# A four-layer graph-attention stack on one core: inverse roots moved to ScalarE, masks planned later, setup products moved to GpSimd

## The chip, the cores and the metric

One Trainium2 chip, of which the kernel uses one core. The metric is the device time of one execution in microseconds (us); the time of a kernel is the median of its runs.

## The reference

128 graphs of 128 nodes go through four attention layers. Each layer is added to its input and normalised over the 512 features. All numbers are float32.

```
def _layernorm(x, axis=-1, eps=1e-5):
    m, v = jnp.mean(x, axis, keepdims=True), jnp.var(x, axis, keepdims=True)
    return (x - m) / jnp.sqrt(v + eps)

# x: (128, 128, 512), adj: (128, 128, 128) of 0 and 1
x = _layernorm(x + L0(x, adj, ...))   # one head: scores x.w_src + x.w_dst + b, softmax over neighbours, attn @ x
x = _layernorm(x + L1(adj, x, ...))   # 4 heads of 256: xl = x @ W1, softmax, + b1, elu; then one head of 512 with W2, + b2
x = _layernorm(x + L2(x, adj, ...))   # 8 heads of 64: h = x @ W, softmax, attn @ h
x = _layernorm(x + L3(x, adj, ...))   # one head: scores from x @ W_fc.T, softmax, elu(attn @ x)

# an attention, e.g. of layer 3
scores = leaky_relu(f1[:, :, None] + f2[:, None, :], 0.2)
scores = where(adj == 0, -1e9, scores)
h_prime = einsum('bnm,bmi->bni', softmax(scores, axis=2), x)
```

## The kernel before

One graph is one tile: its 128 nodes lie on the 128 partitions. A graph passes through some 70 operations in `first`, `second`, `halves` and `third`, and up to sixteen graphs are under way at once. Two passes set the order. `Pipeline.plan` gives each operation of a graph a time, modulo a period of 28 us; graph g's operations get that time plus 28 g. `Pipeline.order` then merges all graphs and the setup into one list: it walks through the operations with one clock for each engine, takes the operation that can start first by the costs written in the code and by `FLOW`, and looks at most 30 us ahead. `FLOW` says how long after its end an operation's result may be read, by the same engine and by others. What is emitted is a fixed order for each engine (PE, DVE, ACT, POOL, and SP for the DMAs); at run time each engine takes its instructions in that order and waits on semaphores. Buffers are placed, and numbered, as the list is emitted.

The steps that the text below speaks of:

- Adjacency matrices are loaded by SP. `mask` turns one into -2^100 or 0 on POOL (L738): m0 for layer 0 (from `ae`, adjacency plus the unit matrix, L838), m2 for layer 2, m3 for layer 3. PE transposes m2 (L850) and DVE multiplies it by `noneye` (L851), which makes m1 for layer 1.
- `spread` writes one column of scores to DRAM and reads it back to all partitions. `attend` takes it: Prelu on ACT (L641), masked scores with the negated maximum nm on DVE (L649), exponential with its sum rs on ACT (L658), reciprocal ri on DVE (L666). `turned` transposes by 32x32 blocks on DVE (L602) and a DMA through DRAM (scr).
- `mixed` is attention times features on PE (L725); L896 and L938 are the same for the four and the eight heads. `resid` adds the input on DVE (L733).
- `project` is a product with weights on PE (L710), w1s with four blocks of 258 columns and wha with two of 273; ACT or DVE evicts PSUM (L717, L715). `halves` multiplies by W2 for two graphs at once with seven products in place of eight (sums on POOL L780, PE L794, evictions L807 on ACT and L812 on DVE).
- `norm`, four in a graph: mean and variance mv by DVE (L676, L677), the inverse root rd by POOL as an addition and a power (L680, L681). The first normalisation is then one DVE operation (L699). For the other three POOL makes the offset mr = -mean x rd (L688, and L692 where 1 is added) and ACT applies scale and offset (L695).
- The setup loads the weights and makes scores' columns from them: `dot2` (L413 and L466) multiplies and sums rows of W2 on DVE, `dots` (L499, L503) rows of the layer-2 weights, and PE sums the W2 columns (L479). The setup's operations stand in the same list as the first graphs'.

Of the kernel before, what the change touches and what calls it, by code (L numbers as in the profile page):

```python
# [17 lines left out]
P = 128  # L18
# [11 lines left out]

PERIOD = 28.0
LATENCY = {"PE": (0.0, 0.8), "DVE": (0.15, 1.6), "ACT": (0.1, 1.6), "POOL": (0.1, 1.6), "SP": (6.8, 6.8)}
FLOW = {"PE": (0.0, 0.6), "DVE": (0.15, 0.9), "ACT": (0.1, 0.9), "POOL": (0.1, 0.9), "SP": (3.2, 3.2)}
AHEAD = 30.0
URGENCY = 0.3
BANKS = 8
# [38 lines left out]
class Pipeline:  # L75
# [69 lines left out]
    def order(self, events):  # L145
# [52 lines left out]
        while len(out) < n:  # L198
            best = None
            for e, waiting in known.items():  # L200
                found = None
                for i in waiting:
                    if events[i][0] > events[low][0] + AHEAD and i != low:
                        break
                    t = start(i)
                    if t is not None and (found is None or t < found[0]):
                        found = (t, i)
                        if t <= clock[e]:
                            break
                if found and (best is None or found < best):  # L210
                    best = found
            t, i = best
            op = ops[i]
            known[op.engine].remove(i)
            issued[i] = True
            out.append((events[i][1], op))
            for b in makes[i]:
                b.slot = free[b.tag].pop(0)[1]
                coming[b.tag].remove(i)
            clock[op.engine] = done = t + op.cost  # L220
            own, other = FLOW[op.engine]
            if op.dma:

                done = lane = max(lane, done) + op.dma
                own = other = FLOW["SP"][0]
            for q in after[i]:
                ready[q] = max(ready[q], done + (own if ops[q].engine == op.engine else other))
                before[q] -= 1
                if not before[q]:
                    insort(known[ops[q].engine], q)  # L230
            for b in op.bufs:
                released[b] = max(released.get(b, 0.0), done + other)
                open_uses[b] -= 1
                if not open_uses[b] and b.slot is not None and b.tag != "const":
                    insort(free[b.tag], (released[b], b.slot))
            while low < n and issued[low]:
                low += 1
# [4 lines left out]
def tile_gat_stack(  # L242
# [44 lines left out]
    nc.vector.tensor_sub(noneye, ones, ident)  # L287
    eye_i = const.tile([P, P], I32, name="eye_i")
    nc.vector.tensor_copy(eye_i, ident)
    neghalf = const.tile([P, 1], F32, name="neghalf")  # L290
    nc.vector.memset(neghalf, -0.5)
    minus = const.tile([P, P], F32, name="minus")
    nc.vector.memset(minus, -1.0)

# [160 lines left out]
        at(40 + s, "PE", 3.5, lambda b=b, f=ones_out: f(b), [w2_marks[0, s], w2_marks[1, s]], [b])  # L455
        at(41 + s, "DVE", 0.33, lambda b=b, f=into: f(b), [b, b2b], [b2b])

    part = const.tile([P, 4], F32, name="part")
    s2 = [spread_row(89, r, 0) for r in r2]
    w2_dots = []  # L460

    def dot2(j, k, s):
        for n in range(2):
            w = w2s[:, SLOT[k // 4, n], k % 4]
            dot(j, w[:, : F // 2], s2[s].ap[:, n * F // 2 : (n + 1) * F // 2], part[:, 2 * s + n : 2 * s + n + 1])
        nc.vector.tensor_add(  # L466
            w2s[:, SLOT[k // 4, s], k % 4, F // 2 : C2], part[:, 2 * s : 2 * s + 1], part[:, 2 * s + 1 : 2 * s + 2]
        )

    for k in range(KH):  # L470
        for s in range(2):
            w2_dots.append(mark())
            j = passing(F)
            at(90 + 2 * k + s, "DVE", 0.9, lambda j=j, k=k, s=s: dot2(j, k, s), [*w2_marks.values(), s2[s]], [j, w2_dots[-1]])

    def shifts(b):
        for s in range(2):
# [15 lines left out]
    at(109.3, "DVE", 1.1, lambda: nc.vector.tensor_sub(w2s[:, 6], w2s[:, 1], w2s[:, 4]), [t2], [t4])  # L493
    w2_ready = [t1, t2, t3, t4]

    def dots(j, k, a, cols):

        pr = j.ap.rearrange("p (h o) -> p h o", h=H2)
        nc.vector.tensor_mul(  # L499
            pr, wha[:, k, :SH].rearrange("p (h o) -> p h o", h=H2)[:, :, :FO],  # L500
            a.ap.rearrange("p (h o) -> p h o", h=H2),
        )
        nc.vector.tensor_reduce(out=wha[:, k, cols], in_=pr, op=ALU.add, axis=AX.X)  # L503

    a3, wf = ([passing(F) for _ in range(2)] for _ in range(2))
    acb, fcp = [passing(P) for _ in range(2)], passing(F)
# [35 lines left out]
    for k in range(KF):  # L542
        for s in range(2):
            for what, cols in ((a3[s], slice(SH + s * H2, SH + (s + 1) * H2)), (wf[s], slice(FO + s, SH, CH))):
                wh_ready.append(mark())
                j = passing(F)
                at(157 + 12 * k + 6 * s, "DVE", 1.2, lambda j=j, k=k, what=what, cols=cols: dots(j, k, what, cols),
                   [*wh_marks[k], what], [j, wh_ready[-1]])

    work = ctx.enter_context(tc.tile_pool(name="work", bufs=1))  # L550
    dram = ctx.enter_context(tc.tile_pool(name="dram", bufs=1, space=bass.MemoryType.DRAM))
# [10 lines left out]
    def graph(g):  # L562
# [107 lines left out]
                ), [zz, ri], [zz])  # L670
            return turned(zz, nh, moving=scaled), ri

        def norm(y, on_act=False, plus=0.0):

            st, mv, rd = small("st", 6), small("mv", 2), small("rd", 1)
            op("DVE", 0.6, lambda: nc.vector.bn_stats(st.ap, y.ap), [y], [st])  # L676
            op("DVE", 0.1, lambda: nc.vector.bn_aggr(mv.ap, st.ap), [st], [mv])  # L677

            def root():
                nc.gpsimd.tensor_scalar_add(rd.ap, mv.ap[:, 1:2], EPS)  # L680
                nc.gpsimd.tensor_tensor(out=rd.ap, in0=rd.ap, in1=neghalf, op=ALU.pow)  # L681

            op("POOL", 0.9, root, [mv], [rd])
            if on_act:
                mr = small("mr", 1)

                def offset():
                    nc.gpsimd.tensor_scalar(  # L688
                        out=mr.ap, in0=mv.ap[:, 0:1], scalar1=rd.ap, scalar2=-1.0, op0=ALU.mult, op1=ALU.mult
                    )  # L690
                    if plus:
                        nc.gpsimd.tensor_scalar_add(mr.ap, mr.ap, plus)  # L692

                op("POOL", 0.6 if plus else 0.3, offset, [mv, rd], [mr])
                op("ACT", 0.6, lambda: nc.scalar.activation(  # L695
                    y.ap, y.ap, AF.Identity, bias=mr.ap, scale=rd.ap
                ), [y, rd, mr], [y])
                return mv, rd
            op("DVE", 0.45, lambda: nc.vector.tensor_scalar(  # L699
                out=y.ap, in0=y.ap, scalar1=mv.ap[:, 0:1], scalar2=rd.ap,  # L700
                op0=ALU.subtract, op1=ALU.mult,
            ), [y, mv, rd], [y])

        def project(lhs, wa, nk, w, t, evict, to, ready):

# [29 lines left out]
            ), [pa, ri, r], [o])  # L735

        def mask(m, a, what):
            op("POOL", 0.8, lambda: nc.gpsimd.tensor_scalar(  # L738
                out=m.ap, in0=a.ap, scalar1=0.0, scalar2=-BIG, op0=what, op1=ALU.mult
            ), [a], [m])  # L740

        def score(xv, wv, init, sc, s):
            jk = Buf("junk", [P, F])
# [167 lines left out]
        def third(g, st, xl2):  # L911
# [6 lines left out]
            pa = mixed(pt, xl2, F)  # L918
            x2 = Buf("x2", [P, F])
            resid(x2, pa, ri, xb)  # L920
            norm(x2, on_act=True)


            xT = turned(x2, KF)
            xl3 = Buf("xl3", [P, C3])
            project(xT, lambda k, c: wha[:, k, c * C3 // 2 : (c + 1) * C3 // 2], KF, C3 // 2, xl3, ["DVE", "ACT"],
                    lambda t, c: t.ap[:, c * C3 // 2 : (c + 1) * C3 // 2], wh_ready)
            db = spread(Col(xl3, SH, H2), H2)
            z3 = Buf("z3", [P, H2, CH])
# [29 lines left out]
                nc.vector.tensor_add(sc4.ap, sc4.ap, xl3.ap[:, C3 - 2 :])  # L959

            op("DVE", 0.2, scores, [z3, xl3], [sc4])
            mv, rd = norm(x3, on_act=True, plus=1.0)

            def normed():

# [18 lines left out]
            ), [e3, pa], [y])  # L984

            op("POOL", 1.3, lambda: nc.gpsimd.tensor_add(y.ap, y.ap, x3.ap), [y, x3], [y])  # L986
            norm(y, on_act=True)
            op("SP", 0.4, lambda: nc.sync.dma_start(out=out[g], in_=y.ap), [y], [], 1.0, dma=0.72)  # L988
        if g == B:

# [60 lines left out]
```

## Time and profile before

| | |
|---|---|
| median of 3 runs | 3205.73 us (3203.74 to 3207.6) |
| profiled execution, own time | 3213.19 us |
| its span, first to last instruction | 3211.2 us |
| mean granted PE clock | 0.980 |
| PE busy (matmuls) | 3050.0 us, 95% |
| DVE busy | 2967.3 us, 92% |
| ACT busy | 2172.0 us, 68% |
| POOL busy | 2285.5 us, 71% |
| DMA, main queue q1 | 75.9% of 16 engines |

Busy times are averages over fill, steady part and drain; the end of a matmul is modelled, so that rows of PE can overlap the next one. Views used below: the list of waits (an engine and line, whom it waited for, total us, times, longest), the table of stretches (busy time of each engine in a stretch of the span), groups by line (count, busy time, mean ns of one), and the timeline (start, length, engine, line, operation).

### The profile page before, as it was taken

To read this page: it belongs to the slowest core of one execution; us is meant where nothing else is said; L and a number is where in the kernel's file an instruction comes from. 1 tells how busy PE (TensorE), PEld (TensorE's weight loads), DVE (VectorE), ACT (ScalarE), POOL (GpSimd) and SP (SyncE) were. 2 spreads that over 40 slices of the span, in tenths; PEclk is the share of its full clock that TensorE was granted. 3 is DMA by queue.
4 is the path that set the end of the run, shared out by engine and by line. 5 is a ranking of instruction groups with operands and counts; after the bars stand their busy time and mean duration, and the time that the engine had idled before them with its cause. 6 is when DMAs were issued, how large, how long until landed. Compare 5 with 4: busy or idle time off the path is not lost. (4 is left out here: it accounts for less than half of the span.)

```text
span 3211.2 us, 62683 instructions
## 1 busy us (share of the span) xinstructions
PE 3050.0 (95%) x14822; PEld 2483.6 (77%) x14822; DVE 2967.3 (92%) x10185; ACT 2172.0 (68%) x7427; POOL 2285.5 (71%) x3211
## 2 busy tenths in 40 slices
PE   7899999999999999999999999999999999999974
PEld 4688877788878878788788787887888878878852
DVE  6978999999999999999999999999999999999985
ACT  1356667677777777777777767777777777777764
POOL 3566777777777777777777777777777777777654
PEclk8999999999999999999999999999999999999985
DMA  4457787787888887888788888887787777878784
GB/s 117 104 147 189 190 196 192 192 202 193 204 192 197 202 194 198 197 197 200 193 198 201 192 203 199 194 204 193 198 200 195 200 197 195 203 190 205 183 192 110
DMA packets 1657572, 606.13 MB, mean 189 GB/s; under 512 B 1311562, under 2 KB 1508170, under 8 KB 1657204
## 3 DMA queue, kind: packets, MB, share of 16 engines
q1 hardware_dynamic: 1655836, 598.97, 75.9%
q8 instruction: 120, 1.97, 0.3%
q14 instruction: 248, 2.03, 0.2%
q0 software_dynamic: 576, 2.10, 0.2%
q10 hardware_dynamic: 792, 1.06, 0.1%
HBM read 374.43 MB, written 227.48 MB: 187 GB/s over the span
## 5 line engine op out<-in xcount | busy, mean ns | idle before, releaser
L658 ACT ACTIVATE w<-w,nm 128x128 f32<-128x128 f32 x1920 | 754.2, 394 | 389.5 <-DVE nm L649 347.3
L710 PE MATMUL ps<-w1s,w 128*128 128x258 f32 x4096 | 940.3, 383 | 7.1 <-DMA w<-scr 7.1
L710 PEld LDWEIGHTS ps<-w1s,w 128*128 128x128 f32 x4096 | 780.7, 191 | 176.8 <-issue 30.0
L794 PE MATMUL ps<-w2s,w 128*128 128x257 f32 x3584 | 872.5, 382 | 8.3 <-POOL w L780 5.8
L649 DVE CUSTOM_DVE_ANT_0 w<-w,w 128x128 f32<-128x128 f32 x1920 | 853.6, 545 | 14.4 <-ACT w L641 12.1
L794 PEld LDWEIGHTS ps<-w2s,w 128*128 128x128 f32 x3584 | 655.7, 190 | 98.1 <-POOL w L780 8.0
L602 DVE STREAM_TRANSPOSE w<-w 128x512 f32<-128x512 f32 (+1 forms) x1024 | 539.2, 540 | 45.9 <-POOL w L668 43.8
L710 PE MATMUL ps<-wha,w 128*128 128x273 f32 x2048 | 518.4, 397 | 4.7 <-DMA w<-scr 4.2
L695 ACT ACTIVATE w<-w,mr,rd 128x512 f32<-128x512 f32 x384 | 311.5, 812 | 298.8 <-POOL mr L688 207.2
L641 ACT ACTIVATE w<-w,xl 128x128 f32<-128x128 f32 x1536 | 480.4, 389 | 35.0 <-DMA w<-row 32.4
L710 PEld LDWEIGHTS ps<-wha,w 128*128 128x128 f32 x2048 | 389.2, 195 | 134.9 <-issue 35.6
L950 POOL TENSOR_TENSOR w<-z,w 128x512 f32<-128x512 f32 x128 | 151.7, 1185 | 348.1 <-DVE z L942 301.1
L680 POOL TENSOR_SCALAR rd<-mv 128x1 f32<-128x1 f32 x512 | 153.3, 299 | 341.2 <-DVE mv L677 184.5
L681 POOL TENSOR_TENSOR rd<-rd,neghalf 128x1 f32<-128x1 f32 x512 | 345.7, 675 | 42.7
L658 ACT ACTIVATION_READ_ACCUMULATOR w<-w,nm 128x1 f32 x1920 | 361.4, 188 | 0.0
L676 DVE BATCH_NORM_STATS2 st<-w 128x6 f32<-128x512 f32 x512 | 340.7, 675 | 10.3 <-POOL w L986 6.3
L717 ACT COPY xl<-ps 128x258 f32<-128x258 f32 (+1 forms) x640 | 226.4, 363 | 153.5 <-PE ps L710 152.7
L881 POOL TENSOR_TENSOR xl<-xl,b1t 128x512 f32<-128x512 f32 x256 | 325.1, 1290 | 0.3
L725 PE MATMUL ps<-w,w 128*128 128x512 f32 x512 | 271.7, 613 | 37.4 <-DMA w<-scr 26.5
L938 PEld LDWEIGHTS ps<-xl,w 128*128 128x128 f32 x2048 | 263.1, 195 | 37.4 <-DVE nm L649 12.8
L649 DVE DVE_READ_ACCUMULATOR2_ANT nm<- 128x1 f32 x1920 | 288.2, 150 | 0.0
L938 PE MATMUL ps<-xl,w 128*128 128x66 f32 x2048 | 256.0, 274 | 18.0 <-DMA w<-scr 11.9
(183 smaller groups left out, 4452.1 us busy)
## 6 DMA issues: line engine op xcount, KB each, us to landing
scr<-w SPq DMA_DIRECT2D x640, 256.0 KB
w<-scr SPq DMA_DIRECT2D x640, 256.0 KB
w<-row SPq DMA_DIRECT2D x128, 512.0 KB
w<-in_x_dram SPq DMA_DIRECT2D x128, 256.0 KB
w<-row SPq DMA_DIRECT2D x128, 256.0 KB
out_dram<-w SPq DMA_DIRECT2D x128, 256.0 KB
w<-row SPq DMA_DIRECT2D x384, 64.0 KB
scr<-w SPq DMA_DIRECT2D x384, 64.0 KB
```

The costliest lines, as they stand in the source:

```text
L602: op("DVE", 0.12 + 0.133 * n, lambda: nc.vector.transpose(zb.ap.rearrange("p b h c -> p h b c"), src.ap.rearrange("p (h b c) -> p h b c", ...
L641: nc.scalar.activation(z.ap[:, h, :], db.ap[:, h0 + h, :], AF.Prelu, bias=src(h0 + h), alpha=SLOPE)
L649: nc.vector.tensor_tensor_reduce(out=zz.ap[:, h, :].rearrange("p (b a) -> p a b", b=4), in0=z.ap[:, h, :].rearrange("p (a b) -> p a b", b= ...
L658: nc.scalar.activation(zz.ap[:, h, :], zz.ap[:, h, :], AF.Exp, bias=nm.ap[:, h : h + 1], scale=-1.0, accum_out=rs.ap[:, h : h + 1],)
L676: op("DVE", 0.6, lambda: nc.vector.bn_stats(st.ap, y.ap), [y], [st])
L681: nc.gpsimd.tensor_tensor(out=rd.ap, in0=rd.ap, in1=neghalf, op=ALU.pow)
L695: op("ACT", 0.6, lambda: nc.scalar.activation(y.ap, y.ap, AF.Identity, bias=mr.ap, scale=rd.ap), [y, rd, mr], [y])
L710: op("PE", w * 4 / 2400 + 0.006, lambda k=k: nc.tensor.matmul(px.ap[:, :w], lhsT=lhs.ap[:, k, :], rhs=wa(k, c), start=(k == 0), stop=(k == ...
L725: op("PE", width * 4 / 2400, lambda: nc.tensor.matmul(pa.ap[:, :width] if len(xv.shape) == 2 else pa.ap.rearrange("p (s c) -> p s c", s=2) ...
L794: return lambda: nc.tensor.matmul(q[b].ap[:, :C2], lhsT=x()[:, k, :], rhs=w2s[:, slot, k, :], start=(fresh and k == 0), stop=(k == 3), ski ...
L881: op("POOL", 1.3, lambda nh=nh: nc.gpsimd.tensor_add(xl.ap[:, nh, : 2 * FH], xl.ap[:, nh, : 2 * FH], b1t[:, nh * 2 * FH : (nh + 1) * 2 * F ...
L938: op("PE", 0.225, lambda u=u, h=h: nc.tensor.matmul(pa.ap[:, u * CH : (u + 1) * CH], lhsT=pt.ap[:, u, :], rhs=xl3.ap[:, h * CH : (h + 1) * ...
```

## The change

- The planner's `FLOW` gives POOL's results to other engines 1.2 us after their end, before 0.9; in `order` an operation on POOL can carry an extra delay, and `mask` carries 2.0 us. The written cost of a mask goes from 0.8 to 0.75.
- `norm` makes the inverse root on ACT as exp(-0.5 ln(var + eps)), two instructions on 128x1, in place of the two on POOL. All four normalisations now take the form with an offset from POOL and an Identity on ACT; `on_act` is gone.
- One table set with both functions is loaded at the start.
- `project` of layer 2 evicts both blocks by ACT.
- In the setup, products of `dot2` and `dots` are made by POOL; the W2 ones are summed by ACT, the others by DVE.

With the number of operations in a graph the planner's random shifts fall on other operations, so the order changes everywhere a little.

```diff
-FLOW = {... "POOL": (0.1, 0.9), ...}
+FLOW = {... "POOL": (0.1, 1.2), ...}
...
             own, other = FLOW[op.engine]
+            if op.engine == "POOL":
+                other += op.extra
...
+    eps = const.tile([P, 1], F32, name="eps")
+    nc.vector.memset(eps, EPS)
+
+    nc.scalar.preload_act_table_set("natural_log_exp_and_others")
...
+    for s in range(2):
+        at(89.5, "ACT", 0.6, lambda s=s: nc.scalar.copy(a2[s].ap, s2[s].ap), [s2[s]], [a2[s]])
     for k in range(KH):
         for s in range(2):
-            at(90 + 2 * k + s, "DVE", 0.9, lambda ...: dot2(j, k, s), [*w2_marks.values(), s2[s]], [j, w2_dots[-1]])
+            at(90 + 2 * k + s, "POOL", 1.3, lambda ...: nc.gpsimd.tensor_tensor(... op=ALU.mult), [*w2_marks.values(), a2[s]], [j])
+            at(91 + 2 * k + s, "ACT", 0.85, lambda ...: nc.scalar.activation(
+                j.ap, j.ap, AF.Copy, accum_out=w2s[:, SLOT[k // 4, s], k % 4, F // 2 : C2]
+            ), [j], [j, w2_dots[-1]])
...
-                at(157 + 12 * k + 6 * s, "DVE", 1.2, lambda ...: dots(j, k, what, cols), [*wh_marks[k], what], [j, wh_ready[-1]])
+                at(157 + 12 * k + 6 * s, "POOL", 1.3, lambda ...: products(j, k, what), [*wh_marks[k], what], [j])
+                at(158.5 + 12 * k + 6 * s, "DVE", 0.65, lambda ...: nc.vector.tensor_reduce(
+                    out=wha[:, k, cols], in_=heads_of(j.ap), op=ALU.add, axis=AX.X
+                ), [j], [wh_ready[-1]])
...
             def root():
-                nc.gpsimd.tensor_scalar_add(rd.ap, mv.ap[:, 1:2], EPS)
-                nc.gpsimd.tensor_tensor(out=rd.ap, in0=rd.ap, in1=neghalf, op=ALU.pow)
-
-            op("POOL", 0.9, root, [mv], [rd])
-            if on_act:
-                ...
-            op("DVE", 0.45, lambda: nc.vector.tensor_scalar(
-                out=y.ap, in0=y.ap, scalar1=mv.ap[:, 0:1], scalar2=rd.ap,
-                op0=ALU.subtract, op1=ALU.mult,
-            ), [y, mv, rd], [y])
+                nc.scalar.activation(rd.ap, mv.ap[:, 1:2], AF.Ln, bias=eps)
+                nc.scalar.activation(rd.ap, rd.ap, AF.Exp, scale=-0.5)
+
+            op("ACT", 0.44, root, [mv], [rd])
+            mr = small("mr", 1)
+            ...
+            op("POOL", 0.6 if plus else 0.3, offset, [mv, rd], [mr])
+            op("ACT", 0.7, lambda: nc.scalar.activation(
+                y.ap, y.ap, AF.Identity, bias=mr.ap, scale=rd.ap
+            ), [y, rd, mr], [y])
...
         def mask(m, a, what):
-            op("POOL", 0.8, lambda: nc.gpsimd.tensor_scalar(
+            op("POOL", 0.75, lambda: nc.gpsimd.tensor_scalar(
                 out=m.ap, in0=a.ap, scalar1=0.0, scalar2=-BIG, op0=what, op1=ALU.mult
-            ), [a], [m])
+            ), [a], [m], 2.0)
...
-            project(xT, lambda k, c: wha[...], KF, C3 // 2, xl3, ["DVE", "ACT"], ...)
+            project(xT, lambda k, c: wha[...], KF, C3 // 2, xl3, ["ACT", "ACT"], ...)
```

## The prediction

> **What bounds the kernel now.** I read the table of stretches first, to separate the steady part from the fill and the drain.
>
> ```profile
> 400.00:800.00 400.00, 387.00 (x1913) 318.16 (x1912) 377.60 (x1297) 280.56 (x963) 295.82 (x421) 1.00 0.80 195
> 800.00:1200.00 400.00, 390.42 (x1934) 320.96 (x1934) 380.27 (x1314) 285.44 (x979) 299.76 (x420) 1.00 0.81 198
> 1600.00:2000.00 400.00, 391.67 (x1935) 321.59 (x1934) 381.87 (x1316) 285.71 (x982) 300.30 (x420) 1.00 0.81 198
> 3100.00:3211.20 111.20, 56.91 (x182) 36.14 (x182) 65.76 (x241) 56.09 (x178) 48.29 (x94) 0.63 0.57 136
> ```
>
> The columns are the stretch, its length, busy us (and instructions) of PE, PEld, DVE, ACT and POOL, the granted clock, the DMA share and GB/s. From 400 to 2800 us nothing changes: PE 98% busy, DVE 95%, ACT 71%, POOL 75%. One step of PE (L725 w<-w,w, timeline) starts at 1600.44 and again, two graphs later, at 1647.80: 47.36 us, so 23.68 us a graph. 128 of them are 3031 us; 180 us are fill and drain.
>
> Who holds PE up comes from the list of waits. The columns are total us, times and longest.
>
> ```profile
> ACT w L658 <- DVE nm L649: 347.3, 421, 12.3
> ACT w L695 <- POOL mr L688: 207.2, 165, 4.4
> PEld ps L850 <- POOL w L738: 111.1, 108, 4.3
> PE ps L850 <- POOL w L738: 61.2, 102, 2.7
> PE ps L725 <- DMA w<-scr: 26.5, 7, 8.8
> ```
>
> The ACT waits are long but ACT has slack. The PE wait is the one that counts: once in nearly every graph the transposition of the mask (L850) waits for the mask from POOL. Asked for 400 to 2800 us alone, PE waited 55.1 us in 94 cases there and under 2 us for everything else together. The timeline of one case, PE and then POOL:
>
> ```profile
> 1625.06 1.02 PE L725 MATMUL ps<-w,w 128*128 128x512 f32 x2
> 1625.91 0.62 PE L710 MATMUL ps<-wha,w 128*128 128x273 f32 x2
> 1626.95 0.33 PE L850 MATMUL ps<-ident,w 128*128 128x128 f32 x1 [0.41 <-POOL w L738]
> 1627.11 1.09 PE L710 MATMUL ps<-wha,w 128*128 128x273 f32 x4
> ```
>
> ```profile
> 1623.83 0.55 POOL L680 TENSOR_SCALAR rd<-mv 128x1 f32<-128x1 f32 x1
> 1624.46 0.57 POOL L681 TENSOR_TENSOR rd<-rd,neghalf 128x1 f32<-128x1 f32 x1
> 1625.12 0.67 POOL L738 TENSOR_SCALAR w<-ae 128x128 f32<-128x128 int32 x1
> 1625.89 0.27 POOL L688 TENSOR_SCALAR mr<-mv,rd 128x1 f32<-128x1 f32 x1
> 1626.23 0.66 POOL L738 TENSOR_SCALAR w<-adj 128x128 f32<-128x128 int32 x1
> ```
>
> POOL works without a break: add, power, the other mask, an offset, then the mask that PE needs, done at 1626.89. PE's twelve L710 matmuls at 1603.09 take 2.76 us, 0.23 each, so the two at 1625.91 end at 1626.37 and PE loses 0.58 us, though the view shows 0.41: the modelled end of a matmul lies about 0.16 us after the next could start. Corrected by that, 102 x (0.60 + 0.16) = **77 us** are lost to this wait. Behind it PE runs at its rate (30 matmuls of 258 columns at 1613.28 in 6.54 us to the next row, 0.218 each), so without it a graph would take about 23.0 us.
>
> **What the Trainium skill says.** "Perfetto Trace Analysis", Identifying the Most-Contended Engine: matmul busy time is a poor measure of distance to the roofline; the trace agrees, the busy 98% hides part of the wait above. "ScalarE: Activation LUTs", What ACT_TABLE_LOAD costs: an ACTIVATE with a pointer bias takes about 280 + 0.833 N ns, with immediates 186, each pointer 93; here 128 elements took 394 (387 by the rule) and 512 with two pointers 812 (800). Its section on table sets says natural_log_exp_and_others holds both exp and ln; no run shows that yet. "SBUF — State Buffer", two separate sides: a GpSimd operation and a VectorE operation with two SBUF inputs exclude each other for a whole instruction; the trace agrees, L649 takes 0.38 us alone and 1.43 at 1607.02 while POOL runs L780.
>
> **The change part by part.**
>
> *Masks reckoned later.* No instruction more or less; the planner takes a mask as 2.0 us (and 0.3) later for other engines. Buffers are numbered as they are placed, about 346 numbers a graph, 0.068 us each. From mask to its PE output there were 26 to 33 numbers (about 2 us) for graphs 20 to 109; in the changed order there are 96 to 154 (6.5 to 10.5 us). POOL would have to run 4 us later against the plan than now for PE to wait. Gain 77 us, less what is late next. PE's other waits are near nothing now, but each had this stop to catch up in; I allow 0.15 us a graph, a fifth of what is removed: 128 x 0.15 = 19, rounded to **15 to 20 back**. Bounds: 0 and all 77.
>
> *Roots to ScalarE.* POOL loses, per graph, 4 x (0.299 + 0.675) = 3.90 us. ACT gains 4 x (Ln 0.281 + Exp 0.187 to 0.281): 1.9 to 2.2 us by the page's price, and Exp waits for Ln, so up to 0.1 more each. No row shows such a pair. Two ACT instructions behind DVE's mv now stand in ACT's order and hold up what follows (exponentials, evictions of PSUM); L695 behind them waits for POOL's offset as before.
>
> *First normalisation on ScalarE.* DVE loses L699, 0.584; ACT gains 0.812 (row L695), POOL an offset, 0.278. *Eviction of xl3*: DVE loses L715, 0.431, ACT gains 0.363 (L717).
>
> Budgets per graph, scaled from 400 to 23.68 us: DVE 22.56 - 1.02 = 21.5; ACT 16.87 + 2.05 + 0.81 + 0.36 = 20.1, up to 20.5; POOL 17.8 - 3.9 + 0.3 = 14.2. Against 23.0 to 23.1 that is 93%, 88%, 62%. PE stays the bound. Without DVE's relief its 22.56 would be 98% of the new period, so that part is worth nothing alone but carries the first. Fewer POOL operations also exclude DVE less; not counted.
>
> *Setup products on POOL.* DVE loses 16 products of w2 (eight stand from 49.19 to 57.29, so 16.2 us in all) and 16 of wha (L499, 1.03 to 1.57: 16 to 25 us). POOL gains 32 of about 1.28 (L862), 41 us; ACT 16 summing passes of about 0.8. PE's L479 needs the last w2 sum and stands ahead of graph 1's projection. Sixteen products and what lies between them (two L862, two masks, sum and offset: 4.6 us) take 25 us from about 48, so L479 opens near 74 where it was served by 69.3. That is **up to 6 us later** for PE; DVE's free 16 us pull graph chains forward by up to as much. Bounds -8 to +8; I take +2. The table load moves from 13.00 to the start, 1.28 us either way: 0, hidden behind the loads of w1.
>
> *Drain.* A norm's chain in the drain changes from add, power (0.23, 0.57 in the chain of work that ended last) to about 0.55 plus one hop: within 3 us, taken as 0.
>
> Sum: -77 + 17 + 2 = -58 on the profiled execution's 3213.2 us; that execution is 7.5 above the median of the runs, so 3205.7 - 58 = 3148; the fill's lean and the lighter POOL are one-sided, I take **3145**.
>
> **The rivals.**
> *ACT becomes the limit (slower, 0.16).* ACT's order is fixed, and of each graph it now idles 23.68 - 16.87 = 6.8 us, mostly waiting for nm (178.6 us in 1600) and mr (160.6). If more than 23.68 - 20.1 = 3.6 us of these waits survive, ACT sets a longer period than now; with 4 us, 24.1 us a graph, 3205.7 + 128 x 0.42 = 3260. For it: four more waits on mv and evictions behind them. Against: the waits exist because ACT is early, and shrink when it is fuller.
> *A new wait takes half (0.12).* A late sum (L794 from POOL) or DVE's 93% costs PE 0.35 us a graph: 3205.7 - 77 + 45 = 3174; at its worst no change (0.06).
> *The change doesn't do what it says.* Were the tables exchanged, eight loads of 1.283 us a graph would add 10 us to ACT. The built order has one load in all, so I give it no chance of its own.
>
> **How the numbers follow.** Likeliest (0.66): 3145, its own range 3110 to 3165. Half gain 0.12, no change 0.06, slower 0.16. Faster 0.78, same 0.06, slower 0.16; 0.2% (6.4 us) is about what a measurement of this kernel can tell from no change. The range 3108 to 3204 leaves out the slower case and little else.
>
> **What would show it.** Right: no row of PE L850 waiting for POOL L738 over 10 us; about 23.1 us between every other L725 of PE; ACT near 87%, DVE near 93%; the sum of PE's waits in 400 to 2800 us under 20. Wrong: ACT over 92% with PE waiting for its evictions (L710 or L938 from ACT), or L850 still waiting; a fill that reaches full rate more than 8 us later.

## The result, and the profile after

The changed kernel takes **3245.14 us** (median of 4 runs, 3239.83 to 3253.06) against 3205.37 us for the kernel before, measured beside it: 1.0126 times as long, 95% interval 1.0099 to 1.0152. The forecast was 3145. Its profiled execution took 3239.83 us with a span of 3237.8, that is 26.6 us over the profiled execution of before; the traces therefore show two thirds of the 39.8 us between the medians, since the one execution lay 5.3 us below its median and the other 7.8 above.

Busy time of the changed kernel, from its page:

```profile
span 3237.8 us, 62168 instructions
PE 3059.5 (94%) x14822; PEld 2501.7 (77%) x14822; DVE 2694.0 (83%) x9833; ACT 2450.4 (76%) x8741; POOL 1902.3 (59%) x2347
```

The work moved as the change says: DVE 273 us and POOL 383 us less, ACT 278 us more. None of the four engines' totals tells why it became slower. The table of stretches, with the columns as in the prediction:

```profile
0.00:400.00 400.00, 359.83 (x1632) 284.07 (x1633) 303.75 (x987) 230.66 (x794) 235.75 (x266) 0.96 0.60 150
800.00:1200.00 400.00, 387.35 (x1914) 321.57 (x1914) 339.73 (x1260) 314.83 (x1128) 242.91 (x301) 0.99 0.80 195
1600.00:2000.00 400.00, 387.39 (x1914) 318.77 (x1912) 337.39 (x1261) 314.07 (x1127) 241.67 (x300) 1.00 0.79 196
```

In the steady part DVE is down to 85%, ACT at 79%, POOL at 60%, and PE is at 387 of 400, where it had 391. No engine but PE is near its limit, and PE's 97% holds waits, as the 98% of before did.

For the **period** one instruction of DVE that occurs once in a graph (L966, sc<-swf,mv,sc) serves as a clock. In before it starts at 718.08 us for the twentieth graph and at 2854.32 for the hundred-and-tenth: 23.74 us a graph. In after it is 715.11 and 2881.28: 24.07. So the twentieth graph comes 3.0 us earlier than before, the ninety graphs after it lose 30 us, and the rest is even. The loss lies in the steady part.

The list of waits of the whole changed kernel (who waited, for whom, total us, times, longest):

```profile
ACT w L646 <- DMA w<-row: 447.7, 261, 6.2
POOL ae L838 <- DMA adj<-in_adj_dram: 275.5, 80, 11.8
DVE w L654 <- ACT w L646: 145.1, 126, 5.3
```

and of PE alone between 400 and 2800 us:

```profile
PE ps L710 <- DMA w<-scr: 35.8, 28, 3.2
PE ps L710 <- DVE nm L654: 13.4, 7, 4.3
PE ps L710 <- DVE w L903: 5.8, 3, 2.6
```

L850, which stood first in the prediction, has 2.1 us left. None of it is for the mask. PE's waits there are 73.7 us in all. About half are for DMAs, and most stand at the third layer's projection (L710), for its transposed input. In before the same wait of ACT for rows (L641 there) was 100.2 us in the whole execution.

For all runs below, **PE's lost time** is counted in one way: between 400 and 2800 us, the gap between the starts of two matmuls less the usual gap of that kind (its lower quartile), wherever more than 0.15 us is left. Before it is 74.9 us, 70.8 of them ahead of L850; after, 103.6, with 92.9 ahead of L710 on wha.

Not all of this is waiting. After some of its stops PE's granted clock stands at 0.50 for 3.4 or 6.8 us, and the matmuls there start about twice as far apart. A case of after, the table of stretches and PE's row:

```profile
1328.10:1334.70 6.60, 4.93 (x11) 3.78 (x12) 4.96 (x19) 4.51 (x20) 4.27 (x5) 0.50 0.56 142
```

```profile
1329.77 6.43 PE L710 MATMUL ps<-wha,w 128*128 128x273 f32 x16 [4.33 <-DVE nm L654]
```

Between 400 and 2800 us such stretches add up to 41.0 us in after and 3.4 in before. The lost time ahead of matmuls for which PE did not wait, nearly all of it in these stretches, is 20 of the 103.6 us in after and 2 of the 74.9 in before. So of the 29 us by which lost time grows, about 18 are matmuls at half clock and 11 are stops. The stops have become fewer and longer: 60 of 1.4 us on average, where before had 97 of 0.75.

### The profile page after: what moved, and what is told of

The parts are those of the page before. It is cut to its first block, busy times and chain, and to the rows that moved or that the text cites. A ratio compares the mean times of both kernels' runs of the same rounds, so it can differ in the third digit from the quotient of the medians.

```text
span 3237.8 us, 62168 instructions
## 1 busy us (share of the span) xinstructions
PE 3059.5 (94%) x14822; PEld 2501.7 (77%) x14822; DVE 2694.0 (83%) x9833; ACT 2450.4 (76%) x8741; POOL 1902.3 (59%) x2347
## 5 line engine op out<-in xcount | busy, mean ns | idle before, releaser
L710 PE MATMUL ps<-w1s,w 128*128 128x258 f32 x4096 | 921.1, 383 | 8.5 <-DMA w<-scr 8.5
L710 PEld LDWEIGHTS ps<-w1s,w 128*128 128x128 f32 x4096 | 779.9, 191 | 129.5 <-DVE wha L551 7.6
L654 DVE CUSTOM_DVE_ANT_0 w<-w,w 128x128 f32<-128x128 f32 x1920 | 741.4, 480 | 156.5 <-ACT w L646 145.1
L794 PEld LDWEIGHTS ps<-w2s,w 128*128 128x128 f32 x3584 | 666.4, 190 | 148.3 <-issue 57.9
L646 ACT ACTIVATE w<-w,xl 128x128 f32<-128x128 f32 x1536 | 487.5, 394 | 256.4 <-DMA w<-row 238.8
L607 DVE STREAM_TRANSPOSE w<-w 128x512 f32<-128x512 f32 (+1 forms) x1024 | 541.3, 539 | 99.6 <-ACT w L699 66.8
L710 PE MATMUL ps<-wha,w 128*128 128x273 f32 x2048 | 532.9, 411 | 83.8 <-DMA w<-scr 48.7
L710 PEld LDWEIGHTS ps<-wha,w 128*128 128x128 f32 x2048 | 393.4, 198 | 223.5 <-ACT w L646 45.2
L699 ACT ACTIVATE w<-w,mr,rd 128x512 f32<-128x512 f32 x512 | 411.6, 808 | 30.1 <-POOL mr L692 18.2
L780 POOL TENSOR_TENSOR w<-w,w 128x512 f32<-128x512 f32 x192 | 245.4, 1286 | 167.8 <-DMA out_dram<-w 56.3
L692 POOL TENSOR_SCALAR mr<-mv,rd 128x1 f32<-128x1 f32 x512 | 183.3, 360 | 271.2 <-ACT rd L686 196.8
L717 ACT COPY xl<-ps 128x258 f32<-128x258 f32 (+1 forms) x768 | 274.7, 364 | 74.1 <-PE ps L710 72.4
L646 ACT ACTIVATE w<-w,sc 128x128 f32<-128x128 f32 x384 | 152.0, 399 | 222.0 <-DMA w<-row 209.0
L938 PEld LDWEIGHTS ps<-xl,w 128*128 128x128 f32 x2048 | 262.4, 196 | 60.0 <-ACT w L663 13.1
L738 POOL TENSOR_SCALAR w<-adj 128x128 f32<-128x128 int32 x256 | 181.6, 709 | 212.6 <-DMA adj<-in_adj_dram 66.0
L725 PE MATMUL ps<-w,w 128*128 128x512 f32 x512 | 271.8, 613 | 26.9 <-DMA w<-scr 23.2
```

Source lines behind the costliest of these rows:

```text
L607: op("DVE", 0.12 + 0.133 * n, lambda: nc.vector.transpose(zb.ap.rearrange("p b h c -> p h b c"), src.ap.rearrange("p (h b c) -> p h b c", ...
L646: nc.scalar.activation(z.ap[:, h, :], db.ap[:, h0 + h, :], AF.Prelu, bias=src(h0 + h), alpha=SLOPE)
L654: nc.vector.tensor_tensor_reduce(out=zz.ap[:, h, :].rearrange("p (b a) -> p a b", b=4), in0=z.ap[:, h, :].rearrange("p (a b) -> p a b", b= ...
L699: op("ACT", 0.7, lambda: nc.scalar.activation(y.ap, y.ap, AF.Identity, bias=mr.ap, scale=rd.ap), [y, rd, mr], [y])
L710: op("PE", w * 4 / 2400 + 0.006, lambda k=k: nc.tensor.matmul(px.ap[:, :w], lhsT=lhs.ap[:, k, :], rhs=wa(k, c), start=(k == 0), stop=(k == ...
L717: op("ACT", 0.06 + w / 1200, lambda: nc.scalar.copy(dst(), px.ap[:, :w]), [px], [t])
```

## The experiments

Each ratio is to the kernel before on the same chip. That took 3212 to 3214 us there, and 3205 where the changed kernel was measured, so a run is compared with the changed kernel by the ratios, each 0.001 of them being 3.2 us. Period and lost time are reckoned as above; half clock is how long the granted clock stood at 0.50 between 400 and 2800 us. "Order kept" means that the planner's list is untouched, and only what an entry emits is changed.

| run | median us | ratio, 95% interval | period us | PE lost us | half clock us |
|---|---|---|---|---|---|
| masks_only | 3207.37 | 0.9987 (0.9975 to 0.9999) | 23.80 | 72.4 | 34.1 |
| before_no_mask_wait | 3207.70 | 0.9987 (0.9980 to 0.9994) | 23.73 | 67.7 | 3.4 |
| before_ln_exp | 3187.95 | 0.9923 (0.9908 to 0.9938) | 23.51 | 52.9 | 3.4 |
| masks_ln_exp | 3194.58 | 0.9951 (0.9931 to 0.9970) | 23.62 | 60.2 | 27.3 |
| before_ln_exp_xl3 | 3185.11 | 0.9915 (0.9898 to 0.9932) | 23.48 | 48.4 | 3.4 |
| before_ln_exp_norm1 | 3263.58 | 1.0162 (1.0147 to 1.0177) | 24.21 | 108.4 | 0 |
| before_all_edits | 3258.61 | 1.0144 (1.0129 to 1.0159) | 24.16 | 103.2 | 0 |
| root_on_pool_same_order | 3304.28 | 1.0285 (1.0261 to 1.0310) | 24.60 | 146.6 | 51.2 |
| after_norm1_on_dve | 3310.66 | 1.0311 (1.0282 to 1.0340) | 24.59 | 154.2 | 102.4 |
| after_rows_later | 3273.76 | 1.0187 (1.0163 to 1.0211) | 24.22 | 111.4 | 17.1 |
| after_loads_on_pool | 3335.06 | 1.0379 (1.0363 to 1.0396) | 24.86 | 175.2 | 92.2 |
| after_no_rows | 3107.34 | 0.9674 (0.9659 to 0.9688) | 22.98 | 0 | 0 |
| before_no_rows | 3192.63 | 0.9940 (0.9925 to 0.9955) | 23.70 | 64.8 | 0 |
| after_rows_unread | 3303.13 | 1.0277 (1.0260 to 1.0294) | 24.67 | 154.7 | 75.1 |
| after_seed3 | 3315.29 | 1.0323 (1.0303 to 1.0344) | 24.67 | 152.5 | 58.0 |
| after_seed14 | 3283.47 | 1.0214 (1.0194 to 1.0234) | 24.47 | 125.0 | 17.1 |
| before_seed38 | 3253.46 | 1.0132 (1.0117 to 1.0148) | 24.10 | 102.9 | 13.7 |
| before_seed53 | 3240.65 | 1.0090 (1.0075 to 1.0105) | 24.02 | 97.6 | 6.8 |

### Is the stop at L850 worth its 77 us? (masks_only, before_no_mask_wait)

masks_only is the kernel before with the planner's part of the change alone:

```diff
-FLOW = {... "POOL": (0.1, 0.9), ...}
+FLOW = {... "POOL": (0.1, 1.2), ...}
+            if op.engine == "POOL":
+                other += op.extra
-            op("POOL", 0.8, ... [a], [m])
+            op("POOL", 0.75, ... [a], [m], 2.0)
```

> The kernel before with only the planner's part of the change: POOL's results 1.2 us later for other engines, masks 2.0 us later still, mask cost 0.75. Same instructions as before. If removing the wait of L850 is worth what the wait is long: wait under 10 us and 3130 to 3160 us. If another wait takes its place as soon as PE no longer stops there (VectorE was 95% busy): wait gone, but 3190 to 3240 us with new waits of PE for something else. If the new planning itself does not reach L850: 61 us of that wait remain and 3205 us.

It redraws the order, so a second run takes the wait away without moving anything:

```diff
-nc.tensor.transpose(pm.ap[:, :P], m2.ap, ident)
+nc.tensor.transpose(pm.ap[:, :P], ident, ident)
```

> The kernel before with its emission order untouched; only the transpose at L850 reads a constant tile instead of the mask m2, so TensorE never waits there (the second mask m1 is then empty; m2 is still made and used in the third layer). This isolates the 77 us of L850. Theory A (the stop at L850 only hid the lateness of the loop over the other in-order queues; TensorE's loss moves elsewhere): 3185 to 3215 us, the L850 wait gone and the sum of TensorE's waits in 400 to 2800 us within 20 us of before. Theory B (my prediction: behind L850 TensorE runs at its rate; masks_only lost it only because the order was redrawn): about 3130 to 3155 us, with under 30 us of TensorE's lost time left.

Both removed the wait and both gained about 5 us. In masks_only PE's lost time went ahead of L940 (L938 in before, the heads, 37.5 us) and the third projection (28.4); some 16 of its 72.4 us are matmuls at half clock. In before_no_mask_wait it went ahead of w1s, W2 and L725. The longest waits of PE, 400 to 2800 us, in masks_only and in before_no_mask_wait:

```profile
PE ps L940 <- DVE w L853: 20.5, 18, 2.4
PE ps L712 <- DMA w<-scr: 8.7, 12, 1.4
```

```profile
PE ps L710 <- DMA w<-scr: 20.0, 36, 1.2
PE ps L794 <- POOL w L780: 12.1, 23, 0.8
PE ps L725 <- DVE nm L649: 8.6, 6, 2.2
```

Of the second run's theories A holds. The stop was the place where PE met work that was late anyway. Without the stop PE runs ahead and meets the lateness a little further on, at places where it had hardly a wait before.

### The roots (root_on_pool_same_order, before_ln_exp, masks_ln_exp)

The first is the changed kernel with this edit, the other two are before and masks_only with its reverse (and the table set loaded at the start). All keep their order.

```diff
-nc.scalar.activation(rd.ap, mv.ap[:, 1:2], AF.Ln, bias=eps)
-nc.scalar.activation(rd.ap, rd.ap, AF.Exp, scale=-0.5)
+nc.gpsimd.tensor_scalar_add(rd.ap, mv.ap[:, 1:2], EPS)
+nc.gpsimd.tensor_tensor(out=rd.ap, in0=rd.ap, in1=neghalf, op=ALU.pow)
```

> The changed kernel with its order kept instruction by instruction (the planner still thinks of ScalarE at 0.44 us), but the inverse root is made by GpSimd with an addition and a power. If the pair of Ln and Exp on ScalarE is what costs (its time, or its place in ScalarE's queue): under 3215 us. If the order of the other instructions is what costs, ScalarE stuck in Prelus whose rows have not landed: still 3235 to 3260 us, the wait of L646 for rows still over 350 us.

> The kernel before with its emission order untouched; only the inverse root is emitted as Ln and Exp on ScalarE instead of add and pow on GpSimd. GpSimd falls by 3.9 us a graph, ScalarE rises by about 2. Theory A (GpSimd's lateness is what the wait at L850 shows, and the pair helps as it did within the changed order, where it was worth 59 us): 3140 to 3175 us, L850 under 20 us. Theory B (the roots have slack in this order): within 10 us of before. Theory C (ScalarE's in-order queue makes the root late behind other Prelus): 3220 us or more.

> masks_only (the kernel before planned with masks later, 3207) with the roots emitted as Ln and Exp on ScalarE, its order untouched. Theory A (each order has its own weak place: here the heads and the third projection, which wait for VectorE, and the shorter root relieves only part): 3175 to 3200 us. Theory B (masks later and the shorter root add up): below 3170 us. Theory C (no gain, since GpSimd has no wait left in that order): 3200 to 3212 us.

The pair on ACT is worth 24 us in before's order, 12 in masks_only's and 51 in the changed kernel's, where it was taken back: everywhere a gain, and never from an instruction less on PE. Two forecasts missed: 3304 is slower than either outcome named for root_on_pool_same_order, and 3188 lies between theories A and B of before_ln_exp. In before_ln_exp no lost time is left at L850 although no mask was planned later: with 3.9 us a graph less in POOL's queue, the mask is ready. DVE then stands at 97%:

```profile
1200.00:1600.00 400.00, 393.73 (x1957) 324.61 (x1956) 386.25 (x1325) 311.08 (x1119) 241.94 (x289) 1.00 0.80 199
```

### The first normalisation and the eviction (before_ln_exp_norm1, before_all_edits, before_ln_exp_xl3, after_norm1_on_dve)

In before's order, at the place of the DVE instruction:

```diff
-op("DVE", 0.45, lambda: nc.vector.tensor_scalar(out=y.ap, ... ), [y, mv, rd], [y])
+op("DVE", 0.45, normed, [y, mv, rd], [y, mr1])   # normed: offset on GpSimd, Identity on ScalarE
```

> The kernel before with its emission order untouched, with Ln and Exp on ScalarE (as in before_ln_exp, 3188) and, in addition, the first normalisation on ScalarE, issued at the place where VectorE's instruction stood. VectorE falls by 0.58 us a graph (from 94% to about 91%). Theory A (VectorE, 97% busy in the steady part, is what holds this order once the roots are off GpSimd): 3150 to 3178 us. Theory B (SyncE's queue and the DMA flights hold it): 3180 to 3195 us. Theory C (the Identity stands in ScalarE's queue behind Prelus that wait for rows and makes the first layer late): 3200 us or more.

The eviction is this edit; before_all_edits has both edits, before_ln_exp_xl3 this one without the normalisation:

```diff
-op("DVE", 0.05 + w / 960, lambda: nc.vector.tensor_copy(dst(), px.ap[:, :w]), [px], [t])
+op("DVE", 0.05 + w / 960, lambda: nc.scalar.copy(dst(), px.ap[:, :w]), [px], [t])   # first half of xl3
```

> The kernel before with its emission order untouched, with all three moves of the change inside a graph: Ln and Exp, the first normalisation and the first half of the xl3 eviction on ScalarE. What it lacks of the changed kernel is the redrawn order (masks later) and the setup products. Theory A (the budgets of the prediction are right and only the redrawn order loses them): 3135 to 3170 us, 75 to 110 us under the changed kernel. Theory B (the edits themselves are what makes the changed kernel late): 3230 us or more. Theory C (the edits are worth what the roots alone are): 3180 to 3200 us.

> The kernel before with its emission order untouched, with Ln and Exp and the first half of the xl3 eviction on ScalarE, without the first normalisation there. before_ln_exp gave 3188, and the eviction moved 5 us in before_all_edits. Theory A (VectorE at 97% limits this order; 0.43 us a graph less on it): 3165 to 3185 us. Theory B (the eviction's place in ScalarE's queue makes the third layer late): 3195 us or more. Theory C (no slack used, none won): 3185 to 3192 us.

And the reverse of the normalisation's edit in the changed kernel's order:

```diff
-nc.scalar.activation(y.ap, y.ap, AF.Identity, bias=mr.ap, scale=rd.ap)   # first norm of a graph
+nc.vector.tensor_scalar(out=y.ap, in0=y.ap, scalar1=mv.ap[:, 0:1], scalar2=rd.ap, op0=ALU.subtract, op1=ALU.mult)
```

> The changed kernel with its emission order untouched; only the first normalisation runs as one tensor_scalar on VectorE again, without its offset on GpSimd and its Identity on ScalarE. Theory A (ScalarE's queue is the place where the changed kernel's chains wait, Identity behind Prelus that wait for rows): 3215 to 3235 us. Theory B (ScalarE has room; the first layer's chain has slack): within 8 us of 3245. Theory C (VectorE gets 0.584 us a graph in a place where it has none): 3255 us or more.

The first normalisation costs 75 us in before's order (3264 against 3188), and one line of DVE's waits between 400 and 2800 us shows where:

```profile
DVE w L604 <- ACT w L707: 177.3, 98, 2.3
```

DVE's next entry for that graph is the transposition of the same tensor (L604, L602 in before), and it stood close behind the normalisation (in before mostly one short entry between them, 0.25 us in the median). With the normalisation on DVE there is no such wait; now DVE stops 1.8 us in nearly every graph (177.3 over 98 times) while POOL and ACT work. The changed kernel, whose planner knew of the trip, has 49.5 us of it (L607 for ACT L699). My theory A of this pair of runs, that DVE's relief would bring 3150 to 3178, is false, and so is the theory that all edits in the old order would reach 3170. The eviction alone moves 3 to 5 us.

Taking the edit back in the changed kernel's order costs 59 us as well. So an undo inside a kept order does not measure an edit's worth; it measures edit and misfit together. That holds for the 51 us of the roots too.

### What holds the changed kernel (after_rows_later, after_loads_on_pool, after_no_rows, before_no_rows, after_rows_unread)

First, results of DMAs planned later, and in a run of its own three loads moved from SP's queue to POOL's, with the order kept:

```diff
-FLOW = {... "SP": (3.2, 3.2)}
+FLOW = {... "SP": (4.2, 4.2)}
```

```diff
-nc.sync.dma_start(out=x0.ap, in_=x[g])      # and adj[g], twice
+nc.gpsimd.dma_start(out=x0.ap, in_=x[g])
```

> The changed kernel with one planner constant changed: results of DMAs are expected 4.2 us after their issue instead of 3.2. If Prelus stand too early in ScalarE's queue and hold up the layer-2 normalisation behind them: the wait of L646 for rows falls from 448 us to under 200, the lost time of PE ahead of L710 on wha falls from about 98 us to under 40, and the time to 3150 to 3190 us. If this is one draw of an order among many: any time from 3170 to 3270, without a link to that wait. If ScalarE's load is the limit: 3235 to 3260 us.

> The changed kernel with its emission order untouched; the loads of x (L834) and adj (L835 and L975), three of the about 30 DMAs a graph on SyncE's queue, are issued by GpSimd instead. Theory A (SyncE's in-order queue is what limits the loop once L850 is relieved): 3205 to 3230 us, the waits for w<-row and w<-scr fall. Theory B (SyncE's queue is busy but not the limit): within 8 us of 3245. Theory C (GpSimd, which then stands behind a full load buffer, becomes late): 3260 us or more.

Both were slower, the first also a little slower than any time named for it. In the first the Prelus' wait for rows in 400 to 2800 us stayed (365 us, 347 without the edit). PE's loss ahead of L710 on wha fell to 22.5 us, under the 40 that the forecast named, but 40.6 came up ahead of w1s and 27.2 ahead of L725: the loss moved once more. In the second POOL has 210 us more work, the Prelus wait longer for rows (427 us against 347), and PE waits 72.5 us for w<-scr against 35.8. Neither shows what the rows cost. This pair does:

```diff
-op("SP", 0.6, lambda: nc.sync.dma_start(out=row..., in_=sT...), [sT], [row], ...)
-op("SP", 0.4, lambda: nc.sync.dma_start(out=db..., in_=row...), [row], [db], ...)
+op("SP", 0.6, lambda: None, [sT], [row], ...)
+op("SP", 0.4, lambda: None, [row], [db], ...)
-z.ap[:, h, :], db.ap[:, h0 + h, :], AF.Prelu
+z.ap[:, h, :], minus, AF.Prelu
```

> The changed kernel with its emission order untouched, without the score rows: the two DMAs of every spread (10 of the about 30 DMAs a graph) are left out, and the Prelus read a constant tile. Theory A (the trips of the rows through SyncE's queue, and ScalarE's Prelus that wait for them, are what limits the changed kernel): 3120 to 3170 us, TensorE's lost time in 400 to 2800 us under 40. Theory B (VectorE's and TensorE's own order limits it): 3215 to 3245 us.

> The same in the kernel before: no DMAs for the score rows, Prelus read a constant tile, order untouched. Theory A (the rows are not what limits the kernel before; VectorE and GpSimd do): 3190 to 3205 us, L850 still waiting 50 us or more. Theory B (the rows limit both kernels): 3120 to 3170 us, with L850 under 25 us.

The table of stretches of after_no_rows:

```profile
1200.00:1600.00 400.00, 400.00 (x2005) 333.41 (x2004) 351.52 (x1334) 333.02 (x1188) 254.30 (x315) 1.00 0.70 161
```

and of before_no_rows, with its one wait of PE between 400 and 2800 us below it:

```profile
1200.00:1600.00 400.00, 391.80 (x1944) 322.20 (x1943) 382.36 (x1317) 284.73 (x980) 302.23 (x424) 1.00 0.66 156
```

```profile
PE ps L845 <- POOL w L733: 48.5, 96, 1.3
```

Both were forecast as theory A, and after_no_rows came out faster than its range. Without rows the changed kernel runs PE at 400 of 400 us with no wait at all, at 22.98 us a graph. The kernel before gains 21 us, stays at 23.70, and still waits for its mask (L845 is L850, L733 is L738): its limit is not the rows, and before_ln_exp shows that POOL's work has a part in it. So the change, edits and new order together, gains 85 us (3192.6 to 3107.3), as long as there are no rows. With them the changed kernel pays about 145 us (ratio 1.0126 against 0.9674).

The last run keeps every DMA and its place and leaves only the Prelus' reading of the rows out (the third change of the diff alone):

> The changed kernel with its emission order untouched and all its DMAs issued as before; only the Prelus read a constant tile instead of the spread score rows, so nothing waits for the rows. after_no_rows, without these DMAs, gave 3107. Theory A (it is the wait: ScalarE's queue stands behind a row that has not landed, and what lies behind the Prelus is late): 3105 to 3130 us. Theory B (it is the load: ten more DMAs a graph on SyncE's in-order queue delay the other transfers): 3190 us or more. Between the two: both have a part.

It is no faster than the changed kernel but about 48 us slower. ACT's wait for rows falls from 347 us to 31 (why these are left is not shown), and PE loses 134.8 us at the same place, L710 on wha:

```profile
ACT w L646 <- DMA w<-row: 31.4, 26, 3.4
```

Theory A falls: with the long wait "ACT w L646 <- DMA w<-row" nearly gone, nothing is won, so it is not by itself what costs. What after_rows_unread still has and after_no_rows has not is ten DMAs a graph in SP's queue, and what they move. That transfers hold each other back in the queue is seen in its own waits, 400 to 2800 us, of before, of after, of after_rows_unread and of after_no_rows:

```profile
SPq L617 <- DMA scr<-w: 5.4, 15, 0.6
```

```profile
SPq L622 <- DMA scr<-w: 156.3, 119, 3.9
```

```profile
SPq L622 <- DMA scr<-w: 160.2, 118, 3.9
```

```profile
SPq L617 <- DMA scr<-w: 49.1, 60, 3.1
```

L617 of before is L622 of after: the reading back of a transposed block, which must wait until its writing (scr) has landed. In before's order the queue hardly ever waits for that landing. In the changed order it stands there 119 times, up to 3.9 us, and everything issued behind it stands too. This is a part of what these lines wait for, though. With every cause counted L617 waits 277 us in before, L622 332 in after, and the same line 366 in masks_only, which takes 3207 us. So the queue's waits are shown, but not that they are what makes the changed kernel slower. A stretch of SP's timeline of after, and PE's in the same microseconds (start, length, engine, line):

```profile
1633.98 0.52 SPq L592 DMA_DIRECT2D row<-sT  x1
1634.60 0.64 SPq L622 DMA_DIRECT2D w<-scr  x1
1635.33 1.09 SPq L592 DMA_DIRECT2D row<-sT  x1
1636.47 0.63 SPq L622 DMA_DIRECT2D w<-scr  x1
1637.20 1.45 SPq L592 DMA_DIRECT2D row<-sT  x1
```

```profile
1637.65 1.02 PE L725 MATMUL ps<-w,w 128*128 128x512 f32 x2
1640.54 0.70 PE L710 MATMUL ps<-wha,w 128*128 128x273 f32 x2 [1.87 <-DMA w<-scr]
```

Writings of rows and readings of blocks alternate in one queue; PE waits 1.87 us for the reading issued at 1636.47, which stood behind the writing of a row with a record of 1.09 us. The trace holds 2026 DMA-issuing instructions of SP between 800 and 2400 us in before, 30 a graph, and their records cover 1348 of the 1600 us; in after 1990 and 1270, in after_no_rows 1393 and 756. These records contain waits, so that they are no measure of issuing alone, but the profile counts them nowhere as busy.

What stays open: why after_rows_unread is slower than after and not just equal to it (about 16 of the 51 us by which its lost time is longer are matmuls at half clock), and whether the ten DMAs cost by their places in the queue or by the load on the DMA engines (busy share 0.79 in after, 0.70 in after_no_rows). Against the load speaks only that before ran at 0.81 with less loss. No run separates the two.

### The draw of the order (after_seed3, after_seed14, before_seed38, before_seed53)

> The changed kernel with another seed of the planner's random shifts (3), all costs as they are. If the cause lies in what the change does to the work: 3235 to 3260 us again, L646 waiting for rows some 450 us. If it lies in the order that seed 1 happens to give: another time by more than 15 us either way, and another place where PE waits.

> The changed kernel with another draw of its planner (SEED 14), nothing else. Seed 1 gave 3245, seed 3 gave 3315. Theory A (the loss is the draw, and draws scatter over some 70 us): anywhere from 3190 to 3320 us, and no nearer than 15 us to 3245 more likely than not. Theory B (the edits make it late in whatever order): 3235 us or more.

> The kernel before with another draw of the planner (SEED 38 instead of 1), nothing else. It tells whether the order of before is a favoured draw. Theory A (it is: draws differ by some 70 us as they did for the changed kernel): 3235 to 3320 us. Theory B (before's order is typical): 3195 to 3225 us.

> The kernel before with a third draw of the planner (SEED 53). Seed 1 gave 3213 on this chip and seed 38 3253. Theory A (seed 1 is a favoured draw): 3230 us or more. Theory B (draws scatter evenly around seed 1): 3160 to 3225 us.

Only the planner's `SEED` differs (1 in the two kernels). Three draws of before give 1.000, 1.013 and 1.009 times the measured kernel, three of after 1.013, 1.032 and 1.021. A draw is worth up to 40 us in the one and 63 in the other, as much as the whole change. The measured draw of before is its best of three, that of after too. The draws of after lie on average 0.015 higher (1.022 against 1.007). That points beyond the one draw, but with three each, scattered this widely and overlapping, it is not shown. Against the average draw of before, the measured changed kernel is 0.5% slower and not 1.3%: before's measured order was a lucky one.

## Why the prediction was wrong

**Masks later: the step that failed.** "Behind it PE runs at its rate ... so without it a graph would take about 23.0 us", and with it the allowance of 0.15 us a graph for what is late next. The wait went as said (2.1 us left, a sign named as right), but where it was taken away alone, in masks_only and before_no_mask_wait, this gained about 5 us, not 57 to 62. In these runs that wait set how long PE stood there, not how long a graph took; PE's full rate behind it was measured while its inputs had the stop as a head start. The reserve should have been reckoned from the other queues, not as a fifth of the gain: in the changed kernel it came to 24.07 - 22.98 = 1.09 us a graph, of which 0.2 are matmuls at half clock.

This step accounts for some 55 us of the 100 between 3145 and 3245. For the rest, by which the changed kernel is slower than before, no single step is shown. **A redrawn order had no term in the sum** at all, and draws alone move either kernel by as much; nor had PE's half clock, about 18 of the 33 us that the longer period costs between 400 and 2800 us. How much the edits cost in a redrawn order is open.

**The 23.0 us themselves were right**, for PE: 22.98 with rows left out. The budgets were close there too: DVE 88%, ACT 83%, POOL 64% in the stretch shown, against 93, 88 and 62. DVE is lower because its long instructions got shorter (those of L649 from 545 ns in before to 468 in after_no_rows, 15 in a graph), which fits POOL being less in the way, named in the prediction and not counted; ACT is lower because its instructions lap over each other: in the stretch shown they add up to 434 us and cover 333 (333.02 / 400 x 22.98 = 19.1 us a graph against 20.1). What the budgets lacked was a line for **the DMAs**: 30 a graph, issued in one order by SP, with waits in it. Leaving ten of them out won 145 us; whether their places in SP's queue or their load costs is open. "PE stays the bound" was said of four engines out of five.

**Roots.** The price held. Groups of after:

```profile
L685 ACT ACTIVATE rd<-mv,eps 128x1 f32<-128x1 f32 x512 | 147.1, 287 | 59.1 <-DVE mv L682 51.7 <-DVE ri L671 5.9
L686 ACT ACTIVATE rd<-rd 128x1 f32<-128x1 f32 x512 | 103.9, 203 | 16.2
```

Ln takes 287 ns and Exp 203, where 281 and 187 to 281 were forecast from the Trainium skill's "ScalarE: Activation LUTs", What ACT_TABLE_LOAD costs; the Exp starts 0.32 us after its Ln. What the page's section on table sets says, that one set holds both, is borne out: the trace has one load.

```profile
L295 ACT ACT_TABLE_LOAD x1 | 1.3, 1283 | 0.7 <-PEq L1037 0.7
```

Their worth was missed in the other direction. I gave POOL's 3.9 us a graph no time; by themselves they gain 24 us in before's order, the best of the parts that were measured alone.

**First normalisation.** Moved DVE time was counted, the trip from DVE over POOL and ACT back to DVE was not; in the old order it costs 75 us, and what it costs in a planned one was not isolated.

**Setup and fill.** +2 us within -8 to +8 was forecast; the twentieth graph is 3.0 us earlier. DVE has 31 us less in the first 400 us (335.13 to 303.75), for 32 to 41 forecast less the sums that stay.

**The rivals.** The slower rival had the sign and not the mechanism: ACT is at 79%, and giving the roots back to POOL is slower. That the time came near its 3260 is luck. The half-gain rival's mechanism, a new late wait, is the nearest to what happened, but it was priced at 0.35 us a graph, and its worst case at no change.

**The signs.** Of those of being right only the end of the wait for the mask came; the period is 24.07 and not 23.1, ACT and DVE stand at 79% and 85%, not 87% and 93%, and PE's waits in 400 to 2800 us add up to 73.7 us, not under 20. Of the three signs of being wrong none came: what went wrong was not among them.

The fastest versions that leave nothing out are before with the roots on ACT alone, 3188, and with the eviction too, 3185; both beat before and after, and they differ by less than their intervals.

## What to carry to other kernels

Before a stop on the busiest engine is priced, let that engine run without it in an order that stays as it is: if the loss comes back elsewhere, the stop was only where lateness became visible. Give the DMAs and the queue that issues them a line in the budget too: trips through memory that cost 21 us in one kernel cost 145 in the other, where DVE and POOL had more room. Look at the length of the stops and not only at their sum, since PE's clock was halved behind most of the long ones here. When a planner redraws the whole order, compare several draws on both sides before a difference as small as their scatter is put down to an edit.

## What was not expected of the hardware

One group of DVE, the same 1920 instructions, in after and in after_seed14:

```profile
L654 DVE CUSTOM_DVE_ANT_0 w<-w,w 128x128 f32<-128x128 f32 x1920 | 741.4, 480 | 156.5 <-ACT w L646 145.1 <-DMA scr<-w 3.5 <-ACT w L663 3.2
```

```profile
L654 DVE CUSTOM_DVE_ANT_0 w<-w,w 128x128 f32<-128x128 f32 x1920 | 1060.8, 646 | 37.8 <-ACT w L646 27.0 <-DMA scr<-w 10.3
```

The mean goes from 480 to 646 ns by the order alone (545 in before, 468 in after_no_rows), so DVE's busy time is not a fixed cost of its instructions. It fits the exclusion of GpSimd and VectorE that the prediction cites from the Trainium skill's "SBUF — State Buffer", two separate sides: in before the instructions of this group that run beside none of POOL's have a median of 377 ns, the 357 that overlap a sum of L780 one of 1422. It does not hold for every operation of POOL: beside a mask alone (L738, 72 cases) the median is 383 ns, although a mask reads SBUF as well. The page speaks of any GpSimd operation that reads SBUF; here the measurement decides.

PE's granted clock goes to 0.50 for 3.4 us at a time, in 26 cases for 6.8. All twenty traces together have 135 such stretches between 400 and 2800 us, and each begins within 5 us after the start of a stop of PE of more than 1 us. Of 32 stops over 3 us 29 have one behind them, of 528 stops of 0.5 to 1.0 us 11. The sixteen matmuls of the case shown with the result take 0.40 us each, where the prediction counted 0.23. after_no_rows, where PE never waits, has no such stretch, and PE's busy time for the same 14822 matmuls is 3020.7 us there and 3059.5 in after. That a long stop brings the low clock fits all of this; no run was made to test it.
